# Block 0's transposed h by 32x32 transposes and transfers, and two steps of block 2 ahead of its first FFN chunk

## The chip, the cores and the metric

The kernel runs on one core of one Trainium2 chip. The core has TensorE (in the profile PE for matmuls, PEld for weight loads), VectorE (DVE), ScalarE (ACT), GpSimd (POOL) and SyncE (SP, which here only issues transfers). Each engine works through its own list of instructions in order, and the lists are coupled by semaphores alone. The metric is the device time in microseconds, the median of several runs.

## The reference

One transformer layer over 8192 tokens of 256 features: chunked linear attention with a decay mask and a gate, a residual and a layer norm, then a gated FFN with 768 hidden features and weights that are integers from -127 to 127, a residual and a second layer norm. Cut to its core:

```python
x = layernorm(x + attn(x)); x = layernorm(x + ffn(x))

# attn: T in chunks of C = 32
Q, K, V = x @ W_q.T, x @ W_k.T, x @ W_v.T
mask = where(i >= j, decay ** (i - j), 0)
S = einsum('bncd,bnkd->bnck', Qc, Kc) * mask
O = einsum('bnck,bnkd->bncd', S, Vc)
out = sigmoid(x @ W_g.T) * O @ W_o.T + x

# ffn
h = silu(x @ wg.T) * (x @ wu.T)
return h @ wd.T          # wg, wu, wd: integers / 127
```

## The kernel before

**Tiling.** The tokens are cut into 16 blocks of 512 (NB = 16, TB = 512). A block lies either with features on the partitions (two slices of 128 features, 512 tokens long; names with a T) or with tokens on the partitions (four groups of 128 tokens, 256 features long). The attention reads x in both layouts from memory; Q and K are folded into one product, y. Its steps for one block are v, y and the gate (each by Strassen's scheme of seven half-size products instead of eight, `seven`, L477), the scores (`attn_scores`, L611), the values times the gate (goT, L634) and the output projection with the residual. `seven` is called in two halves: the first issues four products and their sums, the returned function ("rest") issues the other three. Its inputs are sums of quarters of x or goT, which POOL makes (`token_sums`, L431).

**From attention to FFN.** After the residual, h is normalized and has to be turned, since the FFN wants features on the partitions. It is also split in two, hi in a rounded 32-bit format and lo, the remainder, in 16 bits; each FFN product is then done once with hi and once with lo. There are two ways of turning h. `transpose_h` (L710) lets TensorE transpose eight 128x128 tiles into two PSUM banks (tile pt), from where ACT writes hi and DVE writes lo. `move_h` (L729) lets DVE transpose within 32x32 squares (tile sq) and then has SP issue sixteen transfers of 32 KB that bring the squares to their places (tile hT); `split_h` (L752) then makes hi on ACT and lo on POOL. Before, block 0 and the last block go the first way, blocks 1 to 14 the second. Both sq and hT have one buffer.

**The normalization** also has two forms. `layer_norm` (L329) takes moments on DVE, a square root on ACT, a reciprocal on DVE, and scales on DVE, four times 128x256. `scale_and_shift` (L355) makes columns scale and shift on POOL, and `normalize` (L399) lets ACT apply them. `iterated_scale_and_shift` (L370) does the inverse root wholly on POOL, with a power and one refining step; block 1's h uses it (tiles v_h, y_h, t_h, minus_mean_h, term_h). A square root and a sigmoid need different ACT tables, so each change between them loads one.

**The FFN.** `ffn_up` (L768) takes one of six chunks of 128 hidden features: eight matmuls for gate (fg) and up (fu), hi and lo; even chunks begin with hi, odd ones with lo. ACT takes the sigmoid, DVE multiplies twice, and the product u is split like h, hi on ACT (L803), lo on POOL (L804). `ffn_down` (L816) multiplies back.

**Order.** The work is software-pipelined by hand: the FFN of block b stands beside the attention of block b+2 and the early products of block b+3. The prologue is L892 to L930, the loop L941 to L1026. A planner then orders each engine's list by its own idea of when things are ready, so the order in a list can differ from that in the code. `in_turn` (L293) pins an instruction behind the one that was traced before it on its engine; `in_steady_turn` does so only from the second turn of the loop on. A list, once made, is followed strictly: an instruction that waits holds up all behind it on its engine. In the prologue, block 0's output and norm come at L915, block 1's scores at L916, block 2's early products from L919, the turning of block 0 at L924, the load of the sigmoid table at L925, block 1's output from L927, and block 2's gate at L928. In the loop's first turn, chunk 0 is at L953, the gate's rest and block 3's token sums at L955, chunk 1 at L957, block 2's scores at L958 and the load of block 4's xT at L960.

Of the kernel before, what the change touches and what calls it, by code (L numbers as in the profile page):

```python
# [51 lines left out]
AF = mybir.ActivationFunctionType  # L52
ALU = mybir.AluOpType
# [13 lines left out]
HALF = 0.5  # L67
# [4 lines left out]
def kernel(  # L72
# [15 lines left out]
    nc = tc.nc  # L88
# [4 lines left out]
    NB = NT // TB  # L93
# [26 lines left out]
    def load_xT(b, start=None, pieces=1):  # L120
        xt = xin.tile([P, KD, TB], F32, tag="xT", name=f"xT_{b}")
        src = xT[:, span(b, start)].rearrange("(k p) t -> p k t", p=P)
        n = KD // pieces
        for k in range(0, KD, n):
            queue(start).dma_start(xt[:, k : k + n, :], src[:, k : k + n, :])
        return xt
# [15 lines left out]
    xTs, xns = {}, {}  # L142
# [44 lines left out]
    eps = const.tile([P, 1], F32, tag="eps", name="eps")  # L187
# [105 lines left out]
    def in_turn(ins):  # L293
        tc.keep_in_program_order(ins)
# [75 lines left out]
    def iterated_scale_and_shift(mv, kind, name):  # L370
        on_r, on_dst = kind

        def column(tag):
            return small.tile([P, NG], F32, tag=tag, bufs=2, name=f"{tag}_{name}")

        def times(out, a, b):
            nc.gpsimd.tensor_tensor(out, a, b, ALU.mult)

        def line(out, a, slope, at_0):
            nc.gpsimd.tensor_scalar(out, a, slope, at_0, ALU.mult, ALU.add)  # L380

        v, y, t, minus, shift = map(
            column, ("v", "y", "t", "minus_mean", "term")
        )
        in_turn(
            nc.vector.tensor_scalar(
                v, mv[:, :, 1], 1 / on_dst**2, EPS * (on_r / on_dst) ** 2, ALU.mult, ALU.add
            )
        )
        nc.gpsimd.tensor_tensor(y, v, half, ALU.pow)  # L390
        nc.gpsimd.tensor_scalar(minus, mv[:, :, 0], -1.0, None, ALU.mult)
        times(t, y, y)
        times(t, t, v)
        line(t, t, -0.5, 1.5)
        times(y, y, t)
        times(shift, y, minus)
        return y, shift
# [33 lines left out]
    def token_sums(t, name, order=free):  # L431

        out = sums.tile([P, 4, HB], F32, tag=f"{name[0]}_sums", name=f"{name}_sums")
        t1, t3, t2, t4 = (out[:, i, :] for i in range(4))
        b11, b12, b21, b22 = (t[:, k, n * HB : (n + 1) * HB] for k in range(2) for n in range(2))
        order(nc.gpsimd.tensor_tensor(t1, b12, b11, ALU.subtract))
        nc.gpsimd.tensor_tensor(t3, b22, b12, ALU.subtract)
        nc.gpsimd.tensor_tensor(t2, b22, t1, ALU.subtract)
        nc.gpsimd.tensor_tensor(t4, t2, b21, ALU.subtract)
        return b11, b21, b22, t4, t1, t2, t3  # L440
# [110 lines left out]
    def split_v(b, x_sums):  # L551
        v = work.tile([P, NG, D], F32, tag="v", name=f"v_{b}")
        return v, seven(f"v_{b}", token_major(w_sums["v"], x_sums), by_tokens(v))
# [57 lines left out]
    def attn_scores(b, yT):  # L611
        xt = xTs.pop(b)
        halves = [slice(i * PAIR, (i + 1) * PAIR) for i in range(P // PAIR)]
        ps = bank(f"ps_{b}")[:, : NG * PAIR].rearrange("p (g c) -> p g c", c=PAIR)
        for g in range(NG):
            for fc in range(KD):
                for rows in halves:
                    tokens = slice(g * P + rows.start, g * P + rows.stop)
                    nc.tensor.matmul(  # L619
                        ps[rows, g, :],  # L620
                        lhsT=xt[:, fc, tokens],
                        rhs=yT[:, fc, tokens],
                        start=(fc == 0),
                        stop=(fc == KD - 1),
                    )
        sTs.append(sTs.pop(0))
        sT = sTs[-1]
        for rows in halves:
            in_steady_turn(
                nc.vector.tensor_tensor(sT[rows, :, rows], ps[rows], mask[rows], ALU.mult)  # L630
            )
        return sT.rearrange("p g c -> p (g c)")
# [59 lines left out]
    def attn_out(b, goT):  # L692
        r = attn_residual(b, goT)
        layer_norm(r, f"a{b}", on_r=HALF, on_dst=H_UP)
        return r
# [216 lines left out]
    goT = attn_values(0, sT, v, sg)  # L912
    rest()
    fd = integers(ffn_dT, ffn_int[2], "fd")
    hs[0] = attn_out(0, goT)  # L915
    sT_1 = attn_scores(1, yT)  # L916
    xTs[3] = load_xT(3)
    x_sums = token_sums(xTs[2], "x_2")
    v, rest = split_v(2, x_sums)  # L919
    goT = attn_values(1, sT_1, v_1, sg_1)  # L920
    go_sums = token_sums(goT, "go_1")
    rest()
    yT, rest = split_y(2, x_sums)
    hTs[0] = transpose_h(0, hs[0])  # L924
    in_turn(nc.scalar.activation(table, eps, AF.Sigmoid))  # L925
    rest()
    hs[1], out_rest = split_out(1, go_sums)  # L927
    sg, g_rest = split_gate(2, x_sums)  # L928
    scales_h = iterated_scale_and_shift(out_rest(), of_h, "h_1")
    ahead = yT, v, sg  # L930

# [9 lines left out]
    for b in range(NB - 2):  # L941
        n = b + 2
        m = b + 3
        more = m < NB
        xns[n] = load_xn(n)
        hT = hTs.pop(b)
        uT = [], []
        yT, v, sg = ahead
        steady = b > 0
        if b:  # L950
            normalize(hs[b + 1], *scales_h)
            moving = move_h(b + 1, hs[b + 1])
        ffn_up(b, hT, uT, range(0, 1))  # L953
        if b == 0:
            g_rest()  # L955
            x_sums = token_sums(xTs[m], f"x_{m}")
        ffn_up(b, hT, uT, range(1, 2))  # L957
        sT = attn_scores(n, yT)  # L958
        if m + 1 < NB:
            xTs[m + 1] = load_xT(m + 1)  # L960
        ffn_up(b, hT, uT, range(2, 3))
        if b == 0:

            normalize(hs[b + 1], *scales_h)
            moving = move_h(b + 1, hs[b + 1])
        if not more:
            normalize(r_before, *scales_out)
            store(b - 2, r_before)
        if more:
            v_next, v_rest = split_v(m, x_sums)  # L970
        multiply = ffn_up(b, hT, uT, range(3, 4), held=True)
        if more:
            v_rest()
        multiply()
        goT = attn_values(n, sT, v, sg)
        if scales_out is not None and more:
            normalize(r_before, *scales_out)
            store(b - 2, r_before)
        if b == 0:
            look_up(range(4, n_pieces))  # L980
        if b == 1:
            count = count_wide()
        if more:
            go_sums = token_sums(goT, f"go_{n}")
            y_next, y_rest = split_y(m, x_sums)
        ffn_up(b, hT, uT, range(4, KH))
        r_before = r_out
        if more:
            y_rest()
            sg_next, g_rest = split_gate(m, x_sums)  # L990
            hs[n], out_rest = split_out(n, go_sums)
            g_rest()
            mv_h = out_rest()
            ahead = y_next, v_next, sg_next
            hTs[b + 1] = split_h(b + 1, moving)
            std_h = root_in_turn(mv_h, of_h, f"h_{b}")
            if b:
                mv_before, std_before = mv_out, root_in_turn(mv_out, of_out, f"out_{b}")
            back_to_sigmoids()
            if m + 1 < NB:  # L1000

                x_sums = token_sums(xTs[m + 1], f"x_{m + 1}", in_turn)

            def between():
                return scale_and_shift(mv_h, std_h, of_h, f"h_{b}")

            r_out, mv_out, scales_h = ffn_down(b, uT, hs.pop(b), between)
            if b:
                scales_out = scale_and_shift(mv_before, std_before, of_out, f"out_{b}")
        else:  # L1010

            hs[n] = attn_residual(n, goT)
            mv_h = moments(hs[n], f"a{n}", order=in_turn)
            std_out = root_in_turn(mv_out, of_out, f"out_{b}")
            hTs[b + 1] = split_h(b + 1, moving)
            std_h = root_in_turn(mv_h, of_h, f"h_{b}")
            back_to_sigmoids()
            scales_out = scale_and_shift(mv_out, std_out, of_out, f"out_{b}")
            normalize(r_before, *scales_out)
            store(b - 1, r_before)  # L1020

            inverse(std_h, slice(0, NG), HALF)
            for g in range(NG):
                by_vector(hs[n], g, mv_h, std_h)
            r_out, mv_out, _ = ffn_down(b, uT, hs.pop(b), chunkwise=True)
            scales_out = iterated_scale_and_shift(mv_out, of_out, f"out_{b + 1}")  # L1026


# [216 lines left out]
```

## Time and profile before

| | |
|---|---|
| median of 3 runs | 526.34 us (525.77 to 526.76) |
| the profiled execution | 526.4 us |
| its span, first to last instruction | 524.8 us |
| mean granted TensorE clock | 0.997 |
| TensorE matmuls busy | 517.6 us (99%) |
| DVE, POOL, ACT busy | 389.8, 343.0, 322.3 us |
| transfers, mean over the span | 70 GB/s |
| block 0's residuals added (DVE) | 32.20 to 34.61 us |
| block 0's transposes on TensorE | from 41.64 us |
| first FFN chunk on TensorE | from 48.58 us |

The profile is of one execution; its times count from the span's start. A line of the timeline has the start, the length, the engine with the line of the code, the operation, what it writes and reads with sizes, and, in brackets, how long the engine was idle before and what ended that. The chain of work that ended last is followed backwards from the last instruction. Ends of matmuls are modelled, so the chain, which cuts them to a sequence, is better for lengths on TensorE than the timeline, where neighbours overlap: it has the transposes at 41.81 and the first chunk at 48.83.

### The profile page before, as it was taken

The numbers are of one execution on the slowest core, as the hardware profiler recorded it, in microseconds if no ns is written. First come the engines' busy times: TensorE is split into PE (matmuls) and PEld (weight loads), VectorE is DVE, ScalarE is ACT, GpSimd is POOL, SyncE is SP. The second block draws the span as 40 slices with busy tenths as digits, with TensorE's granted clock in tenths as the row PEclk, the third lists the DMA queues.
The fourth block names the chain that finished last, engine by engine and source line by source line (L and its number), as shares of the span: only waits on it lengthen the run. The fifth ranks groups of instructions, "written<-read, shape, count | busy, mean of one in ns | idle before, by whom it ended". The sixth has DMA issues, their size and how long they took to land.

```text
span 524.8 us, 10553 instructions
## 1 busy us (share of the span) xinstructions
PE 517.6 (99%) x3646; PEld 422.3 (80%) x3646; DVE 389.8 (74%) x964; ACT 322.3 (61%) x644; POOL 343.0 (65%) x476
## 2 busy tenths in 40 slices
PE   8999999999999999999999999999999999999995
PEld 4798887887978789787888878879787888878684
DVE  3868797676776867868677776867868677787876
ACT  2754655475655766666665665656567566667745
POOL 6535785776857669486685856678486685835564
PEclk9999999999999999999999999999999999999998
DMA  8631111212313131121311413141131311102112
GB/s 259 197 107 41 49 42 46 67 41 56 108 30 91 49 112 42 38 91 51 105 42 43 120 25 97 44 116 43 33 91 51 110 42 39 44 21 61 44 38 84
DMA packets 43256, 36.90 MB, mean 70 GB/s; under 512 B 4800, under 2 KB 39104, under 8 KB 43200
## 3 DMA queue, kind: packets, MB, share of 16 engines
q1 hardware_dynamic: 42240, 35.41, 23.0%
q10 hardware_dynamic: 960, 0.79, 0.4%
q8 instruction: 30, 0.49, 0.4%
q14 instruction: 26, 0.21, 0.1%
HBM read 20.45 MB, written 8.39 MB: 55 GB/s over the span
## 4 chain that ended last, share of the span: by engine, by line
PE 96%; DVE 2%; ACT 1%; POOL 1%; issue 0%; DVEq 0%; ACTq 0%
PE fg L779 16%; PE fu L779 16%; PE fdn L666 14%; PE p_v L465 9%; PE p_y L447 9%; PE p_g L447 9%; PE p_o L465 8%; PE po L640 5%; PE ps L619 3%; PE fdn L845 2%; PE pa L666 1%; PE pg L561 1%; PE pi L183 1%; PE pv L599 1%; PE py L578 1%; DVE st_f L314 0%
## 5 line engine op out<-in xcount | busy, mean ns | idle before, releaser
L804 POOL TENSOR_TENSOR u_lo<-u,u_hi 128x512 f16<-128x512 f32 (+1 forms) x98 | 123.0, 1257 | 111.1 <-ACT u_hi L803 109.6
L803 ACT CAST u_hi<-u 128x512 fp32r<-128x512 f32 (+1 forms) x98 | 59.7, 609 | 65.3 <-DVE u L801 64.9
L789 DVE SCALAR_TENSOR_TENSOR s<-fg,s 128x512 f32<-128x512 f32 (+1 forms) x98 | 65.8, 673 | 34.3 <-ACT s L787 34.1
L787 ACT ACTIVATE s<-fg 128x512 f32<-128x512 f32 (+1 forms) x98 | 56.9, 583 | 41.5 <-PE fg L779 41.4
L801 DVE TENSOR_TENSOR u<-fu,s 128x512 f32<-128x512 f32 (+1 forms) x98 | 66.4, 678 | 10.4 <-POOL u_lo L804 1.1
L779 PE MATMUL fg<-hT_hi,fg_hi 128*128 128x512 f32 (+1 forms) x196 | 74.0, 458 | 0.0
L779 PE MATMUL fu<-hT_hi,fu_hi 128*128 128x512 f32 (+1 forms) x196 | 60.5, 390 | 0.0
L779 PE MATMUL fg<-hT_lo,fg_lo 128*128 128x512 f16 (+1 forms) x196 | 58.0, 377 | 0.0
L779 PE MATMUL fu<-hT_lo,fu_lo 128*128 128x512 f16 (+1 forms) x196 | 57.4, 375 | 0.0
L666 PE MATMUL fdn<-fd_hi,u_hi 128*128 128x256 f32 x312 | 46.9, 292 | 0.0
L779 PEld LDWEIGHTS fu<-hT_hi,fu_hi 128*128 128x128 f32 x196 | 36.5, 188 | 8.5
L402 ACT ACTIVATE h<-h,shift_h,scale_h 128x256 f32<-128x256 f32 x52 | 27.0, 590 | 24.1 <-POOL shift_h L365 24.1
L779 PEld LDWEIGHTS fg<-hT_hi,fg_hi 128*128 128x128 f32 x196 | 34.6, 189 | 8.8
L666 PEld LDWEIGHTS fdn<-fd_hi,u_hi 128*128 128x128 f32 x312 | 39.8, 189 | 0.3
L666 PE MATMUL fdn<-fd_lo,u_lo 128*128 128x256 f16 x312 | 38.6, 273 | 0.0
L779 PEld LDWEIGHTS <-fu_lo 128*128 128x128 f16 x196 | 19.2, 98 | 22.2
L827 DVE SCALAR_TENSOR_TENSOR r<-fdn,h 128x512 f32<-128x512 f32 x30 | 20.7, 689 | 21.6 <-PE fdn L666 19.1
L762 POOL TENSOR_TENSOR hT_lo<-hT,hT_hi 128x512 f16<-128x512 f32 x28 | 35.2, 1279 | 1.2 <-ACT hT_hi L761 1.2
L779 PEld LDWEIGHTS <-fg_lo 128*128 128x128 f16 x196 | 15.3, 98 | 20.6 <-issue 12.9
L666 PEld LDWEIGHTS <-u_lo 128*128 128x128 f16 x312 | 28.4, 98 | 4.2
L465 PE MATMUL p_v<-v_sums,x_sums 128*128 128x128 f32 x240 | 31.7, 275 | 0.0
L640 PE MATMUL po<-sT,v 128*128 128x128 f32 x256 | 31.2, 275 | 0.0
(207 smaller groups left out, 1183.4 us busy)
## 6 DMA issues: line engine op xcount, KB each, us to landing
x<-in_x_dram SPq DMA_DIRECT2D x16, 512.0 KB, 3.5
xT<-in_xT_dram SPq DMA_DIRECT2D x15, 512.0 KB, 4.2
hT<-sq SPq DMA_DIRECT2D x224, 32.0 KB, 1.9
out_dram<-r SPq DMA_DIRECT2D x14, 512.0 KB, 4.5
fg_int<-in_ffn_gT_dram SPq DMA_DIRECT2D x3, 256.0 KB, 8.4
fu_int<-in_ffn_uT_dram SPq DMA_DIRECT2D x3, 256.0 KB, 7.1
fd_int<-in_ffn_dT_dram SPq DMA_DIRECT2D x3, 256.0 KB, 5.8
xT<-in_xT_dram SPq DMA_DIRECT2D x2, 256.0 KB, 4.2
```

The lines of the kernel that those rows point to most:

```text
L402: nc.scalar.activation(r[:, g, :], r[:, g, :], AF.Identity, bias=shift[:, g : g + 1], scale=scale[:, g : g + 1],)
L447: nc.tensor.matmul(pb, lhsT=a[i - 1], rhs=b[i - 1], start=first, stop=True, skip_group_check=True,)
L465: nc.tensor.matmul(pb[:, g * P : (g + 1) * P], lhsT=b[i - 1][:, g * P : (g + 1) * P], rhs=a[i - 1], start=first and g == 0, stop=True, ski ...
L640: nc.tensor.matmul(po[:, cols], lhsT=v[:, g, dc * P : (dc + 1) * P], rhs=sT[:, cols], start=True, stop=True,)
L666: nc.tensor.matmul(pb[:, j * D : (j + 1) * D], lhsT=part[:, g * P : (g + 1) * P], rhs=w, start=(i == 0), stop=(i == len(terms) - 1),)
L762: nc.gpsimd.tensor_tensor(in_order[1], whole, in_order[0].bitcast(F32), ALU.subtract)
L779: nc.tensor.matmul(pb, lhsT=w[kind][:, dc, hc * P : (hc + 1) * P], rhs=hT[kind][:, dc, cols], start=(kind == kinds[0] and dc == 0), stop=( ...
L787: order(nc.scalar.activation(s, pg, AF.Sigmoid, scale=SCALE / H_UP))
L789: gated = nc.vector.scalar_tensor_tensor(s, pg, U_UP / H_UP**2, s, ALU.mult, ALU.mult)
L801: in_steady_turn(nc.vector.tensor_tensor(u, pu, s, ALU.mult))
L803: nc.scalar.copy(hi, u)
L804: nc.gpsimd.tensor_tensor(lo, u, hi.bitcast(F32), ALU.subtract)
```

## The change

Block 0 goes the way of the other blocks. A table load for the square root comes first; `attn_residual`, the moments, `root` and `scale_and_shift` take the place of `attn_out`; after block 2's first v products ACT normalizes, loads the sigmoid table, and `move_h` issues transposes and transfers. `split_h` comes after block 2's first gate products, where hTs[0] is now made.

In the loop's first turn the gate's rest, block 3's token sums, block 2's scores and the load of block 4's xT come before chunk 0 instead of after chunks 0 and 1. In later turns their order is as it was.

Three more instructions on POOL are pinned: in `iterated_scale_and_shift` the power (behind whatever was traced before it) and the negated mean (behind the power), for every use of it; and in `token_sums` the second sum, t3, wherever the caller gives an order. That is so at the end of each turn, and now in the first turn too.

```diff
-        nc.gpsimd.tensor_tensor(y, v, half, ALU.pow)
-        nc.gpsimd.tensor_scalar(minus, mv[:, :, 0], -1.0, None, ALU.mult)
+        in_turn(nc.gpsimd.tensor_tensor(y, v, half, ALU.pow))
+        in_turn(nc.gpsimd.tensor_scalar(minus, mv[:, :, 0], -1.0, None, ALU.mult))
...
         order(nc.gpsimd.tensor_tensor(t1, b12, b11, ALU.subtract))
-        nc.gpsimd.tensor_tensor(t3, b22, b12, ALU.subtract)
+        order(nc.gpsimd.tensor_tensor(t3, b22, b12, ALU.subtract))
...
-    hs[0] = attn_out(0, goT)
+    in_turn(nc.scalar.activation(table, eps, AF.Sqrt))
+    hs[0] = attn_residual(0, goT)
+    mv_h = moments(hs[0], "a0")
+    std_h = root(mv_h, "a0", HALF)
     sT_1 = attn_scores(1, yT)
+    scales_h = scale_and_shift(mv_h, std_h, of_h, "h_0")
     xTs[3] = load_xT(3)
     x_sums = token_sums(xTs[2], "x_2")
     v, rest = split_v(2, x_sums)
+    normalize(hs[0], *scales_h)
+    in_turn(nc.scalar.activation(table, eps, AF.Sigmoid))
+    moving = move_h(0, hs[0])
     goT = attn_values(1, sT_1, v_1, sg_1)
     go_sums = token_sums(goT, "go_1")
     rest()
     yT, rest = split_y(2, x_sums)
-    hTs[0] = transpose_h(0, hs[0])
-    in_turn(nc.scalar.activation(table, eps, AF.Sigmoid))
     rest()
     hs[1], out_rest = split_out(1, go_sums)
     sg, g_rest = split_gate(2, x_sums)
+    hTs[0] = split_h(0, moving)
     scales_h = iterated_scale_and_shift(out_rest(), of_h, "h_1")
...
-        hT = hTs.pop(b)
...
+        else:
+            g_rest()
+            x_sums = token_sums(xTs[m], f"x_{m}", in_turn)
+            sT = attn_scores(n, yT)
+            xTs[m + 1] = load_xT(m + 1)
+        hT = hTs.pop(b)
         ffn_up(b, hT, uT, range(0, 1))
-        if b == 0:
-            g_rest()
-            x_sums = token_sums(xTs[m], f"x_{m}")
         ffn_up(b, hT, uT, range(1, 2))
-        sT = attn_scores(n, yT)
-        if m + 1 < NB:
-            xTs[m + 1] = load_xT(m + 1)
+        if b:
+            sT = attn_scores(n, yT)
+            if m + 1 < NB:
+                xTs[m + 1] = load_xT(m + 1)
```

## Prediction

> **What bounds the kernel now.** I read the page's busy shares first, then the chain of work that ended last around the edit, then busy time by stage.
>
> ```profile
> PE 517.6 (99%) x3646; PEld 422.3 (80%) x3646; DVE 389.8 (74%) x964; ACT 322.3 (61%) x644; POOL 343.0 (65%) x476
> ...
> 34.00:42.00 8.00, 8.00 (x88) 7.67 (x87) 6.99 (x19) 3.34 (x7) 1.88 (x3) 1.00 0.39 133
> 48.00:54.00 6.00, 6.00 (x41) 4.18 (x41) 4.83 (x17) 2.71 (x6) 3.74 (x7) 1.00 0.27 87
> ```
>
> The columns of the last two lines are the stage, its length, then busy time of PE, PEld, DVE, ACT and POOL, granted clock, DMA share and GB/s. TensorE has no gap in either stage: each microsecond of matmul taken away there is a microsecond of the kernel, and each microsecond for which TensorE waits is added. The other four engines have room. The chain in order of time says the same, and gives the pieces the edit touches (start, length, what):
>
> ```profile
> 41.81 0.87 PE pt L718 x8
> ...
> 48.83 0.47 PE fg L779 x2
> ...
> 50.21 0.43 PE fu L779 x2
> 50.64 1.29 PE p_g L447 x6
> ...
> 53.73 1.08 PE ps L619 x32
> ```
>
> So the eight transposes of block 0 cost TensorE 0.87 us. The first chunk of block 0's FFN runs 48.83 to 50.64 (1.81 us), the gate's rest takes 1.29, block 2's scores 1.08.
>
> The new way of moving h is already used for blocks 1 to 14. Block 2's move, in the timeline:
>
> ```profile
> 83.53 0.20 POOL L365 TENSOR_TENSOR shift_h<-mv_a,minus_h 128x4 f32<-128x4 f32 x1
> 83.76 2.08 ACT L402 ACTIVATE h<-h,shift_h,scale_h 128x256 f32<-128x256 f32 x4 [3.14 <-POOL shift_h L365]
> ...
> 84.39 1.92 DVE L737 STREAM_TRANSPOSE sq<-h 128x256 f32<-128x256 f32 x4 [0.85 <-ACT h L402]
> ...
> 86.39 11.32 SPq L744 DMA_DIRECT2D hT<-sq  x16
> ```
>
> And the split that follows it, of block 1, with the landing time of all such transfers from the view of tile sq:
>
> ```profile
> 76.04 1.12 ACT L761 CAST hT_hi<-hT 128x512 fp32r<-128x512 f32 x2
> ...
> 78.34 2.52 POOL L762 TENSOR_TENSOR hT_lo<-hT,hT_hi 128x512 f16<-128x512 f32 x2
> ...
> DMA to landing us min/median/max: 1.8/1.9/3.7
> ```
>
> To be seen: first DMA issue 2.63 us after the normalization starts; sixteen issues one behind another on SP, 11.3 us here (10.34, 11.06, 10.73, 10.19 for the other four of the first five, median 10.7); 1.9 us from an issue to its landing; then 0.6 us for the first hi half and 2.5 us for both lo halves. In blocks 1 to 14 some 24 us lie between normalization and first use. Block 0 hasn't got them.
>
> **What the Trainium skill says.** "VectorE: DVE Perf Modes", The three transpose paths: VectorE transposes only inside 32x32 blocks. So the rest of the move is the DMAs' work, sixteen per block here. "DMA: Bandwidth & Descriptors", Bandwidth: transfers under 64 KB are governed by their descriptors, not their bytes. The trace agrees: 32 KB each, 0.6 us of SP each. "ScalarE: Activation LUTs", What ACT_TABLE_LOAD costs: about 1283 ns; the trace has 1.28 us at 36.04. "TensorE: Matmul & The Clock Gate", Part 1: after an idle window of about 3.4 us the clock is halved. The trace shows only the warm-up: the four L183 matmuls of 128x512 start 0.86 us apart where such steps later take 0.43.
>
> **The change part by part.**
>
> Transposes gone from TensorE: -0.87 us. With them go two ACT reads of pt (1.08 us) and two DVE lo halves (1.29), off the path.
>
> Normalization moved from VectorE to ScalarE: four L338 (2.02 us) and one L336 off DVE; four ACTIVATEs (2.08) onto ACT, three small POOL operations. Table loads stay two, one moved forward to about 33 us, when ACT has been through the fd casts and idles until 35.65; one table activation (0.20) is new. Hidden by ACT's idle time; without it, about 2.3 us of delay, not on TensorE's queue.
>
> When does h leave? The last aggregate ends at 35.88, the root takes 0.30 with its table already there, ready by about 36.3. The reciprocal is held behind block 1's second masking (35.91 to 36.34), so 36.37 to 36.55. Three POOL operations take 0.58 (83.15 to 83.73 in the trace of before), so the normalization starts at 37.2. First issue 2.63 later: 39.8. Attention's goT multiply (0.69) becomes ready in the midst of the transposes and can get between them: from 0 to 1.0, I take 0.4. First issue 40.2.
>
> Sixteen DMAs on SP, otherwise empty from 35.6 to 48.5: the last is issued 10.1 us after the first (10.7 less its own 0.6), 50.3, and lands 1.9 later, 52.2. The first hi half 0.61: 52.85. Two lo halves on POOL 2.52: 55.4. What of chunk 0 then remains, three steps of 0.22: chunk 0 ends at 56.05.
>
> What is queued behind these waits: behind each transpose on DVE goT, v and y of the early products; behind the hi casts on ACT the gate's sigmoids; behind the lo halves on POOL, now by an explicit pin, block 1's power and all its scale chain, and behind that block 3's token sums. Delay before chunk 0 costs nothing as long as TensorE still arrives before h, so the lost 0.87 us of cover between y's two halves (copies and p57 may come late by up to 0.5) is free.
>
> The order of TensorE: it would arrive at chunk 0 at 48.83 - 0.87 + 1.29 + 1.08 = 50.33. Before, the same set (chunk 0, gate's rest, scores) was done at 48.83 + 1.81 + 1.29 + 1.08 = 53.01. Now 56.05. Net so far **+3.0 us**: a stall of 3.9 less 0.87.
>
> The pins on POOL: pow starts at 55.4, 1.05; minus 0.2; five small ones at 0.28 apiece, done 58.05; then t1, t3, t2 at 0.74, t2 at 60.3. TensorE, after chunks 1 and 2 (1.79 each), needs t2 after v's first product (0.45): 60.1. So +0.2 to +0.3 there. At worst a u_lo (1.28) gets in ahead: +1.5. In blocks 1 on, pinning t3 puts it behind the lo halves instead of ahead (it ran at 77.66, before 78.34): same POOL total, and TensorE never waited. In the tail minus goes behind pow in the chain at 507: same work, 0 to 0.1.
>
> The steps moved ahead. The gate's rest issues three ACT operations (0.38, 0.42, 0.63), two DVE sums and the token sums. The ACT ones may queue behind the hi casts until 53.5 and end at 55; their first user, block 2's attention multiply, ran at about 64. The scores issue two DVE maskings (0.43 each), used as late. The load of block 4's xT is released by the scores and goes onto SP behind the sixteen issues, which end at about 51; before it was issued at 54.85, and its user comes 25 us later. Block 3's x load, at 48.46 before, may wait on SP until 51 too; its user comes at about 75. Tiles sq and hT have one buffer each: block 1's transposes (60.0) and transfers (62.4) need block 0's landed (52.2) and split (55.4). All at nothing, with 2 us or more to spare.
>
> Sum: -0.87 + 3.9 + 0.3 = **+3.3**. The profiled execution took 526.4 (span 524.8), the median is 526.34: predicted **529.6**.
>
> **The rivals.**
>
> A, likeliest, as above: +3.3; with the first issue from 39.8 to 40.8, the issue train from 10.2 to 11.3 and the sums' stall from 0 to 0.4, +2.1 to +4.6. Chance 0.47.
>
> B, the planner lets other matmuls into the gap. The first products of v, y and g of block 3 read the raw xT (0.45, 0.43, 0.43 us), chunk 2's hi products 0.93. They aren't pinned. For it: in the old schedule t3 ran ahead of the lo halves, so the planner thinks these late. Against it: nowhere in the old trace does TensorE run ahead of its program order. Gives +1.0 to +2.4; 528.2. Chance 0.25.
>
> C, A and something on top: the u_lo ahead of the sums, or the clock halved. The longest unbroken idle is 2.5 us, below the skill's window, but TensorE is busy for only 0.9 in 5. An estimate from the page: half speed for 3.4 us, +1.7. Gives 531.2 to 532. Chance 0.17.
>
> D, not slower: the move is hidden. Place: SP's sixteen issues. It decides if the last lands by about 48.5, so that both lo halves are there when chunk 0 wants them (51.5); that needs the train to take under 7 us, where the trace never shows less than 10.2. Price: -0.87, 525.5. Chance 0.08. The last 0.03 is for disturbances I don't see.
>
> That the pins fail to hold the order (scores behind chunk 0 again) would only lengthen the stall; it is in C.
>
> **How the numbers follow.** Within 0.2% (1.05 us) is about what a measurement of this kernel can't tell from no change. A, C and nearly all of B are above it: slower 0.88. D is 0.16% below before, so it counts as the same: 0.09 with B's lower edge. Faster needs more than the 0.87 that is there to be had: 0.03. For 8 in 10 I leave out D (0.08), B's lowest third (0.08) and C's upper end (0.04): 527.8 to 531.8. A's own range is 528.4 to 530.9.
>
> **What would show it.** No pt on TensorE. ACT normalizing h of block 0 at about 37, before the sigmoid table. SP issuing hT from about 40.2 to 51. ACT's hT_hi at about 52.2, waiting for the DMA. TensorE idle before the first fg of block 0 at about 50.3 to 52.9, and a second time, for hT_lo on POOL, until 55.4. Block 3's x_sums finished about 61 instead of 56.15. The prediction is wrong if the hT issues end before 47, if TensorE runs block 3's products in that gap, or if the difference to before grows again after 62, in stages I called covered.

## The result, and the profile after

The changed kernel takes 532.59 us (median of 5 runs, 531.88 to 533.75) against 526.54 beside it: ratio 1.0122, interval 1.0111 to 1.0134. The forecast was 529.6 with a range of 527.8 to 531.8; the sign was right, and 3 us were missing. The profiled execution took 532.59 (span 530.95; before 526.4 and 524.81), so 6.1 us are to be found in the span. They lie in two places, 470 us apart.

**The first place is block 0's first chunk.** From the page of the changed kernel, the busy shares; then the same two stages as in the prediction and three short ones (stage, length, busy time of PE, PEld, DVE, ACT, POOL, granted clock, DMA share, GB/s), and last two of the short ones in the kernel before:

```profile
PE 518.2 (98%) x3638; PEld 421.5 (79%) x3638; DVE 391.6 (74%) x961; ACT 322.7 (61%) x649; POOL 345.7 (65%) x481
```

```profile
34.00:42.00 8.00, 8.00 (x81) 7.67 (x78) 7.18 (x20) 5.76 (x14) 3.47 (x8) 1.00 0.44 140
48.00:54.00 6.00, 3.78 (x42) 2.42 (x41) 3.40 (x14) 2.36 (x5) 1.69 (x2) 0.97 0.50 148
...
53.00:55.00 2.00, 1.38 (x5) 0.56 (x5) 0.00 (x0) 0.60 (x2) 2.00 (x3) 0.65 0.94 340
55.00:57.00 2.00, 2.00 (x6) 0.62 (x5) 0.77 (x2) 0.60 (x1) 1.75 (x6) 0.50 0.03 8
57.00:58.00 1.00, 1.00 (x6) 0.77 (x5) 0.61 (x1) 0.00 (x0) 0.92 (x4) 1.00 0.00 0
```

```profile
53.00:55.00 2.00, 2.00 (x37) 1.52 (x36) 0.65 (x2) 1.32 (x3) 2.00 (x4) 1.00 0.03 8
55.00:57.00 2.00, 2.00 (x12) 1.27 (x12) 1.39 (x4) 1.00 (x2) 1.84 (x7) 1.00 0.49 94
```

From 48 to 54 TensorE is busy for 3.78 of 6 us, where before it had no gap; and from within 53:55 until 57 it runs at half its clock, which it had not done before. The timeline shows block 0's h on its way:

```profile
37.00 2.08 ACT L402 ACTIVATE h<-h,shift_h,scale_h 128x256 f32<-128x256 f32 x4 [0.27 <-POOL shift_h L365]
...
39.85 10.34 SPq L744 DMA_DIRECT2D hT<-sq  x16
...
51.62 1.14 ACT L761 CAST hT_hi<-hT 128x512 fp32r<-128x512 f32 x2 [3.05 <-DMA hT<-sq]
...
52.29 1.02 PE L779 MATMUL fg<-hT_hi,fg_hi 128*128 128x512 f32 x2 [2.19 <-ACT hT_hi L761]
...
52.31 2.51 POOL L762 TENSOR_TENSOR hT_lo<-hT,hT_hi 128x512 f16<-128x512 f32 x2 [4.33 <-ACT hT_hi L761]
...
54.87 0.59 PE L779 MATMUL fg<-hT_lo,fg_lo 128*128 128x512 f16 x1 [0.62 <-POOL hT_lo L762]
```

And the chain of work that ended last (start, length, what) runs through SP's queue, the last transfer, both halves of the split, and into products of which a pair takes 0.85, twice the usual 0.43:

```profile
49.59 1.85 DMA hT<-sq
...
52.31 2.52 POOL hT_lo L762 x2
54.83 0.04 issue
54.87 0.59 PE fg L779
55.46 0.85 PE fu L779 x2
56.31 0.84 PE fg L779 x2
57.15 0.43 PE fu L779 x2
```

By block 0's products back (fdn) the loss is 3.53 us, before and then after in the chain:

```profile
76.28 5.52 PE fdn L666 x48
```

```profile
79.81 5.52 PE fdn L666 x48
```

Block 0's output projection (tile pa) starts at 30.43 before and 30.20 after in the chain, so from pa to fdn it is 45.85 us before and 49.61 after. It stays there: the last compute of all, the copy of n_wide, comes 3.58 later.

```profile
521.62 0.13 DVE L1179 CAST n_wide<-count 1x1 int32<-1x1 f32 x1
```

```profile
525.20 0.13 DVE L1189 CAST n_wide<-count 1x1 int32<-1x1 f32 x1
```

**The second place is behind the last compute**, where the span goes on for 3.06 us before and 5.61 after, 2.6 us more. Behind n_wide every engine loads that number and branches over the code for wide integers (`tc.If`, L1183 before, L1193 after). The view of that line, before and then after (count, shortest, median and longest in ns, start):

```profile
L1183 ACTq COMPARE_BRANCH  x1: 45/45/45, 522.5 to 522.5; - x1
...
L1183 PEldq COMPARE_BRANCH  x1: 445/445/445, 522.6 to 522.6; - x1
```

```profile
L1193 ACTq COMPARE_BRANCH  x1: 45/45/45, 526.1 to 526.1; - x1
...
L1193 PEldq COMPARE_BRANCH  x1: 3658/3658/3658, 526.2 to 526.2; - x1
```

TensorE's branch takes 3.66 us instead of 0.45, and the other engines wait for it at the end. "Runtime: NRT & Kernel Launch", Instruction fetch mechanics, in the Trainium skill, says that instructions are fetched 16 KB at a time, in sequence, and that a taken branch to a place not among the loaded ones has to wait for a fetch. It gives no time. The trace agrees as far as it shows fetches: the DMA view of the 8 us ahead of TensorE's branch has one on TensorE's instruction queue before,

```profile
q8 instruction: 1, 0.02, 1.0%
```

and none after the change; there two follow the start of the branch, where before it was one (view from 526.2 to 531):

```profile
q8 instruction: 2, 0.03, 2.9%
```

(Columns: fetches, MB, share. The view doesn't name the engine of q8. Over the whole trace it has 30 fetches, 0.49 MB, one for some 245 of TensorE's records, and it is taken for TensorE's queue from that.) The change takes transposes from TensorE: its stream has 16 records fewer, 3638 matmuls and as many weight loads instead of 3646. So the theory to test: **the stream's length moves the branch against the fetches, and the 2.6 us have nothing to do with h.** The rival: something moved by the change (pins, loads) makes the end late. For the first place the theory is the late h, and on top of it the half clock.

### The profile page after: what moved, and what is told of

Its sections match the earlier page's. It is cut to its first block, busy times and chain, and to the rows that moved or that the text cites. A ratio compares the mean times of both kernels' runs of the same rounds, so it can differ in the third digit from the quotient of the medians.

```text
span 531.0 us, 10574 instructions
## 1 busy us (share of the span) xinstructions
PE 518.2 (98%) x3638; PEld 421.5 (79%) x3638; DVE 391.6 (74%) x961; ACT 322.7 (61%) x649; POOL 345.7 (65%) x481
## 4 chain that ended last, share of the span: by engine, by line
PE 90%; DVE 3%; SPq 2%; POOL 1%; DMA 1%; ACT 1%; issue 0%; DVEq 0%; ACTq 0%
PE fg L779 16%; PE fu L779 15%; PE fdn L666 14%; PE p_v L465 8%; PE p_y L447 8%; PE p_g L447 8%; PE p_o L465 8%; PE po L640 5%; PE ps L619 3%; PE fdn L845 2%; SPq L744 2%; PE pa L666 1%; DMA wg<-in_w_gT_dram 1%; PE pg L561 1%; PE pv L599 1%; PE py L578 1%
## 5 line engine op out<-in xcount | busy, mean ns | idle before, releaser
L787 ACT ACTIVATE s<-fg 128x512 f32<-128x512 f32 (+1 forms) x98 | 55.7, 581 | 41.4 <-PE fg L779 40.2
L402 ACT ACTIVATE h<-h,shift_h,scale_h 128x256 f32<-128x256 f32 x56 | 29.1, 590 | 26.2 <-POOL shift_h L365 26.2
L762 POOL TENSOR_TENSOR hT_lo<-hT,hT_hi 128x512 f16<-128x512 f32 x30 | 37.7, 1279 | 9.3 <-ACT hT_hi L761 9.3
```

The costliest lines, as they stand in the source:

```text
L402: nc.scalar.activation(r[:, g, :], r[:, g, :], AF.Identity, bias=shift[:, g : g + 1], scale=scale[:, g : g + 1],)
L762: nc.gpsimd.tensor_tensor(in_order[1], whole, in_order[0].bitcast(F32), ALU.subtract)
L787: order(nc.scalar.activation(s, pg, AF.Sigmoid, scale=SCALE / H_UP))
```

## Experiments on the end

**Length restored in the warm-up.** `idle` is a tile of zeros, `pi` the warm-up's bank.

```diff
+    for _ in range(4):
+        nc.tensor.matmul(pi[:, :32], lhsT=idle[:, :P], rhs=idle[:, :32], start=True, stop=True)
```

> The changed kernel with four float32 matmuls of 128x32 added to the warm-up, so that TensorE's stream has again the 3646 matmul and 3646 weight-load records of the kernel before. They run in the first microseconds, where TensorE has nothing else to do. Theory (the branch): the end of the changed kernel is 2.65 us longer only because TensorE's closing branch took 3.66 us instead of 0.45, and that depends on the length of the stream alone; here the branch is back near 0.45 us, the stretch from the last compute (n_wide) to the end near 3.05 us, and the time at about +3.5 us over the kernel before (530.0, ratio 1.0067). Rival (the tail comes from the pins on GpSimd, or from the moved loads): the stretch stays at 5.7 us and the time at +6 us (ratio 1.0115).

Measured: 533.45 us, ratio 1.0143 (1.0126 to 1.0161), branch 3.54 us. A miss: as many matmuls as before, and a long branch still.

**Length cut in the kernel before.** It leaves out the second half of the features in the scores of block 15's first 256 tokens.

```diff
+                if b == NB - 1 and g < 2 and fc:
+                    continue
...
-                        stop=(fc == KD - 1),
+                        stop=(fc == KD - 1 or (b == NB - 1 and g < 2)),
```

> The kernel before, with a part of the computation left out: the second half of the features in the scores of block 15's first 256 tokens (four float32 products), so that TensorE's stream is 8 matmul and 8 weight-load records shorter, as the changed kernel's is. Nothing of the change is in it. Theory (the branch): the closing branch takes about 3.66 us and the stretch behind the last compute about 5.7 us, which with about 0.2 us of work left out gives +2.4 us (529.0, ratio 1.0046). Rival (the change itself causes the tail): the stretch stays at 3.05 us and the time at -0.2 us (ratio 0.9996).

Measured: 528.68 us, ratio 1.0042 (1.0027 to 1.0057), branch 3.78 us. As the theory says, and against the rival: 16 records of matmuls and weight loads fewer in the kernel before, nothing else of the change, cost 2.6 us net between the medians (528.68 and 526.1).

**Five instead of four in the warm-up.**

> The changed kernel with five instead of four float32 matmuls of 128x32 in the warm-up. The padded kernel with four kept the long branch (3.54 us) and has 7378 records on TensorE's two queues; the kernel before and the filled one have 7379 and a short branch (0.45 and 0.46 us). Theory (the length of TensorE's stream decides, and the step lies between 7378 and 7379): here there are 7382, the branch takes about 0.45 us, the stretch behind n_wide about 3.05 us, and the time is +3.4 us over the kernel before (529.5, ratio 1.0064; 1.005 to 1.0075). Rival (the branch depends on what the changed part does, and the filled kernel shortened it by its faster part): the branch stays near 3.6 us and the ratio at 1.0115 to 1.014.

Measured: branch 0.455 us, with a fetch ahead of it. But 531.64 us, ratio 1.0088 (1.0073 to 1.0103): only part of the gain. The timeline says why: the small matmuls aren't free, and in this execution the eight products behind them took 5.60 us instead of 3.82 in the changed kernel; pa came 3.5 us later than there (33.69 in the chain). TensorE was at the half pace of the warm-up until about 11 us: the weight loads of these products start 0.85 us apart up to 10.80 and 0.43 apart from 11.40, and the clock's record has it full from 11.1, where the changed kernel has it from 5.8. It doesn't always go so: with six small matmuls, in the kernel below that moves h alone, the products took 3.68.

```profile
5.25 2.18 PE L185 MATMUL pi<-idle 128*128 128x32 f32 x10
7.25 5.60 PE L563 MATMUL pg<-xT,wg 128*128 128x512 f32 x8
```

That was a fault of the experiment: padding needs a place where TensorE is really free. Behind its last product it is, for some 3 us.

```diff
+    last = bank("last")
+    for _ in range(5):
+        in_turn(nc.tensor.matmul(last[:, :32], lhsT=idle[:, :P], rhs=idle[:, :32], ...))
     n_wide = const.tile([1, 1], I32, tag="n_wide", name="n_wide")
```

> The changed kernel with five float32 matmuls of 128x32 behind TensorE's last product, where it only waits for n_wide (7382 records, as in the kernel with five in the warm-up). In the warm-up they were not free: block 0's first product behind them (pa) began 0.1 to 3.5 us later than in the changed kernel, and the times fell into two groups 2 us apart. Theory (the branch costs 2.65 us of the change's 6.2, the pads in the warm-up cost the rest): branch 0.45 us, one group of times, +3.5 us over the kernel before (529.9, ratio 1.0067; 1.0055 to 1.0075). Rival (the spread belongs to the changed kernel): two groups again, a median ratio of 1.009.

Measured: 532.33 us, ratio 1.0125 (1.0109 to 1.014), branch 3.40 us. A miss again, though the stream has the records of the kernel with five in the warm-up. Ten, and then seven, in the same place:

> The changed kernel with ten instead of five small matmuls behind the last product (7396 records before the branch against 7376). Theory (the fetch of the next 16 KB of instructions comes ahead of the branch once the stream is long enough): a fetch on TensorE's instruction queue some 8 us before the branch, branch 0.45 us, +3.5 us over the kernel before (529.6, ratio 1.0067; 1.0055 to 1.008). Rival (only records ahead of the fetch's place count, and those behind the last product don't): as with five, branch 3.4 us and ratio 1.0125.

> The changed kernel with seven small matmuls behind the last product (7384 records before the branch), to place the step between five (7376, long) and ten. Theory (a step at a fixed number of records): short (0.45 us) if the step lies below 7384, as the kernels with 7380 and 7381 records and a short branch say. Rival (records behind the last product don't count): long (3.4 us).

Ten: 530.2 us, ratio 1.0073 (1.006 to 1.0085), branch 0.445. Seven: branch 3.52 (one run, 533.49 us).

```profile
L1198 PEldq COMPARE_BRANCH  x1: 445/445/445, 528.1 to 528.1; - x1
```

All kernels together, in the order of the records (matmuls, weight loads and the few others) that TensorE has in the trace ahead of its branch; the first expectations, with 7378 and 7379, count six behind it as well:

| kernel | records | fetch in the 8 us ahead | branch, us |
|---|---|---|---|
| changed; before, cut | 7356; 7357 | no | 3.66; 3.78 |
| four in the warm-up; two queues | 7372 | no | 3.54; 3.78 |
| before; filled | 7373 | yes | 0.45; 0.46 |
| five in the warm-up | 7376 | yes | 0.46 |
| five at the end; sums first | 7376 | no | 3.40; 3.49 |
| order alone; pins alone | 7377 | yes | 0.45; 0.45 |
| x later; early and vector; h alone | 7380; 7380; 7381 | yes | 0.46; 0.45; 0.45 |
| seven at the end | 7384 | no | 3.52 |
| ten at the end, both kernels | 7396 | yes | 0.45; 0.46 |

In all 17 kernels a fetch ahead of the branch and a short branch go together. Among the kernels with nothing added at the end, the longer streams (from 7373 on) have it and the shorter ones (up to 7372) not, so the kernel before stood within a few records of the step. What is shown is that records which compute nothing decide 2.1 to 2.4 us (the changed kernel without and with ten: medians 532.59 and 530.2; each set against the kernel before beside it, +6.05 and +3.9). What stays open is the rule of the step: 7384 records were not enough with seven matmuls at the end, where 7373 were in the kernel before. Something that this count misses takes part.

## Experiments on the wait for h

**The wait filled.** Four float32 matmuls between the scores and chunk 0.

```diff
+            fill = bank("fill")
+            for _ in range(4):
+                in_turn(nc.tensor.matmul(fill, lhsT=idle[:, :P], rhs=idle, start=True, stop=True))
         hT = hTs.pop(b)
```

> The changed kernel with four float32 matmuls of 128x512 (of the warm-up's constants, into a bank that nobody reads) between block 2's scores and block 0's first chunk, where TensorE waited 2.19 us. The stream has the length of the kernel before, as in the padded kernel. Theory (the clock): the half clock from about 53 to 58 us, about 1.2 us of the stall, came of TensorE's idle stretch; with the stretch filled the products of chunk 0 run at 0.21 us from the start, and the time is about 1.2 us below the padded kernel's: +2.3 us over the kernel before (ratio 1.0044). Rival (the clock falls there whatever TensorE does, or the filling takes as long as it saves): the same as the padded kernel, +3.5 us (ratio 1.0067).

Measured: 529.15 us, ratio 1.0057 (1.0044 to 1.007). The branch is short here, so the kernel to set beside it is the one with ten at the end: 1.05 us between the medians, though the intervals of the two ratios overlap. The filled kernel's stages:

```profile
53.00:55.00 2.00, 2.00 (x8) 0.98 (x7) 0.00 (x0) 0.83 (x2) 2.00 (x2) 1.00 1.02 360
55.00:57.00 2.00, 1.99 (x10) 1.10 (x9) 0.74 (x2) 0.60 (x1) 1.83 (x6) 1.00 0.09 31
```

Full clock throughout, with useless work: TensorE's idling cost about 1 us beyond the idling itself. The traces agree: from pa to fdn it is 48.63 us here, against 49.61 in the changed kernel, in whose chain the three pieces at half clock are 0.37, 0.42 and 0.41 longer, 1.2 us. The price isn't the same in each execution: in the five kernels that only have small matmuls added, from pa to fdn it is 48.8 to 51.3 us.

The ratio is above the expected 1.0044, mostly because the kernel with a short branch is itself at +3.8 us and not at +3.5. The filling's length costs little: it runs on until 53.94, while h's first half was ready at 52.5, but TensorE comes to the second low half at 55.10, and POOL has it ready at 55.06 (chain, then timeline):

```profile
55.10 0.01 issue
55.12 0.38 PE fg L779
```

```profile
52.54 2.52 POOL L762 TENSOR_TENSOR hT_lo<-hT,hT_hi 128x512 f16<-128x512 f32 x2 [4.34 <-ACT hT_hi L761]
```

**h's new way alone**, with the gate's rest and the scores back at their places behind chunks 0 and 1:

> The changed kernel with six small matmuls in the warm-up (short branch) and with the gate's rest and block 2's scores back at their places of the kernel before, behind chunks 0 and 1. Theory (the moved work is what covers the transfers): 1.5 us of the gate's rest and 1.15 us of scores no longer lie in the wait, so the wait at the first chunk grows from 2.2 to about 4.8 us and the time is +6.0 us over the kernel before (ratio 1.0114; 1.009 to 1.0135). Rival (the planner finds other work for the wait, or the order is worth nothing): as the kernel with five small matmuls, +3.4 us (ratio 1.0064).

Measured: 535.24 us, ratio 1.0172 (1.0146 to 1.0197). The wait is the 4.8 that was expected, nearly; the time is 3 us more than expected. Its four runs lie at 533.56, 533.88, 536.6 and 537.06, and the profile is that of the second.

```profile
52.78 0.79 PE L781 MATMUL fg<-hT_hi,fg_hi 128*128 128x512 f32 x1 [4.55 <-ACT hT_hi L763]
```

```profile
55.00:57.00 2.00, 1.96 (x5) 0.92 (x4) 0.40 (x1) 0.60 (x1) 1.86 (x5) 0.50 0.00 0
57.00:59.00 2.00, 2.00 (x6) 1.48 (x5) 0.76 (x3) 0.40 (x2) 0.59 (x3) 0.50 0.00 0
```

The half clock is longer here too: it lasts from 52.4 (mean 0.94 in 48:53) to 59.2 (0.95 in 59:61), 6.8 us; in the changed kernel from 53.6 to 57.0, 3.4 us. In the profiled execution of the kernel with ten at the end it was 6.8 us as well (54.2, from 0.79 in 53:55, to 61.0, from 0.75 in 60:62), and that run took 532.03 us where the five others took 529.83 to 531.57, three of them under 529.9. So a longer wait isn't needed for it. The six small matmuls in the warm-up of h alone may have added to its upper two runs.

In all eight traces that have a half clock at this place it lasts 3.4 or 6.8 us. The changed kernel's own five runs fit this: those with a mean granted clock of 0.994 took 531.88 to 532.59, those with 0.991 took 533.44 and 533.75. (In the kernel with ten at the end one run of 531.57 has 0.997 and doesn't fit.) In the clock's record of all 17 traces the stretches at full clock, too, are multiples of 3.41 us long: in seven of the eight the clock falls 47.8 us, 14 times 3.41, after it first rose. So the clock seems to change only at every 3.41 us counted from its first rise, and the place of the wait between two such points may decide how long the half clock is. No run here moves the one against the other alone, so that is not shown.

So the moved work covers 2.4 us of the wait (2.19 against 4.55), and the change without it would be worse.

**The two other parts alone,** each in the kernel before with one small matmul at the end.

> The kernel before with the three instructions on GpSimd pinned, as the change pins them, and nothing else of it (one small matmul behind the last product keeps TensorE's stream at no less than 7379 records). Theory (the pins decide nothing by themselves; the changed kernel's end waits 0.2 us for u_lo at the last products because of them): 0 to +0.2 us, branch 0.45 us (ratio 1.0 to 1.0005). Rival (the pins order GpSimd worse in every block): +1 us or more (ratio 1.002).

> The kernel before with the gate's rest, block 3's token sums, block 2's scores and the load of xT put ahead of block 0's first chunk, h still moved by TensorE (one small matmul behind the last product). Theory (the new order itself costs nothing; the loss is in how h is moved): -0.3 to 0 us, as three switches between the scores and chunk products fall away (ratio 0.9994 to 1.0). Rival (the later start of the chunks leaves VectorE and GpSimd idle, and u or the sums come late): +0.4 us or more (ratio 1.0008).

Measured: pins 526.5 us, ratio 1.0006 (0.9997 to 1.0014); order 526.6, ratio 1.0006 (0.9998 to 1.0015). Neither differs measurably from no change; the pins' rival (1.002) is excluded, that of the order (1.0008) isn't. The pins' trace has one wait more than that of before, 0.2 us at the very last products, as all kernels with the pins have it:

```profile
PE fdn L1092 <- POOL u_lo L804: 0.2, 1, 0.2
```

From pa to fdn it is 45.86 us in both traces, as before (45.85). With that, the loss in block 0 belongs to the late h, since only the kernels that move h have the wait for it.

## Experiments on what makes h late, and a faster version

**Two queues.** ACT's queue issues five of the sixteen transfers (`issue_later` takes them from a list).

```diff
-    moving = move_h(0, hs[0])
+    moving = move_h(0, hs[0], [(2, 3)] + [(3, j) for j in range(4)])
...
     rest()
+    issue_later(2)
     hs[1], out_rest = split_out(1, go_sums)
     sg, g_rest = split_gate(2, x_sums)
+    issue_later(3)
```

> The padded kernel, with five of block 0's sixteen transfers issued from ScalarE's queue (two behind y's rest, three behind the gate's copies) and eleven from SP's. Theory (the stall is the length of the queue: sixteen issues in 10.34 us, 0.65 us apart): the last transfer lands about 3.2 us earlier, the casts begin at about 48.5 to 49.5 us, TensorE waits under 1 us, the clock is not halved, and the time is about +0.4 us over the kernel before (ratio 1.0008; 0.9995 to 1.002). Rival (the transfers themselves or VectorE's squares are what is late, or the two queues slow each other): the stall stays, +2.5 to +3.5 us (ratio 1.005 to 1.0067).

Measured: 532.62 us, ratio 1.0138 (1.0108 to 1.0168). A miss. SP's part was over early, yet h came no earlier. The timeline of this kernel, and the landing times of block 0's tile hT (us, shortest, median, longest):

```profile
40.50 7.13 SPq L753 DMA_DIRECT2D hT<-sq  x11
...
46.64 1.94 ACTq L760 DMA_DIRECT2D hT<-sq  x3
...
48.00 0.37 SPq L131 DMA_DIRECT2D x<-in_x_dram  x1
...
52.31 1.14 ACT L771 CAST hT_hi<-hT 128x512 fp32r<-128x512 f32 x2 [3.08 <-DMA hT<-sq]
```

```profile
DMA to landing us min/median/max: 1.9/1.9/4.2
```

SP, free at 47.6, sent off the next thing in its list: block 3's x, 512 KB. The last small transfers, issued until 48.6, then took up to 4.2 us instead of 1.9 (longest for block 0 in the changed kernel: 2.4). A faster queue had started what it collided with, if this reading is right. Block 3's x held back until block 1's transfers are issued, the load of block 4's xT pinned where it is traced, and six small matmuls in the warm-up in place of four:

```diff
-        xns[n] = load_xn(n)
+        xns[n] = load_xn(n, order=in_turn if b == 1 else free)
...
-            xTs[m + 1] = load_xT(m + 1)
+            xTs[m + 1] = load_xT(m + 1, order=in_turn)
```

> The kernel with two queues, with six small matmuls in the warm-up in place of four (short branch), and with block 3's x, whose load SP issued at 48.0 us between the transfers on ScalarE's queue, held behind block 1's transfers. In the kernel with two queues the last issue was over at 48.6 us but the first cast came at 52.3. Theory (the x load of 512 KB took the DMA engines while the last three transfers were on their way: 4.2 us to landing instead of 1.9): the casts begin at 50.3 to 50.7 us, TensorE waits about 0.5 to 1 us, the clock stays full, and the time is +0.9 us over the kernel before (ratio 1.0017; 1.0005 to 1.003). Rival (two queues slow each other, whatever else moves): casts near 52.3 us, +3.3 us (ratio 1.0063).

Measured: 529.29 us, ratio 1.0047 (1.0029 to 1.0065). In its trace, which is 3.1 us behind that of the two queues from the warm-up on (again the small matmuls), the last issue was over at 51.65, ACT's last three landed in 1.9 us at most, and the cast followed in 1.4 us instead of 3.7:

```profile
49.71 1.94 ACTq L760 DMA_DIRECT2D hT<-sq  x3
...
53.09 1.14 ACT L771 CAST hT_hi<-hT 128x512 fp32r<-128x512 f32 x2 [0.80 <-DMA hT<-sq]
```

So the collision was the cause. The time missed its mark, by the warm-up and by a wait of 0.84 us for POOL's second low half, behind which the clock stayed full. Next, ACT's issues earlier and that half on DVE:

> As the kernel before this one in the list, with the five transfers on ScalarE's queue earlier (three behind y's rest, one behind the p_o copies, one behind the p_g copies) and block 0's second low half computed on VectorE instead of GpSimd (about 0.65 us there against 1.28). Theory (all the loss of the changed kernel but the branch is the late hT): the casts begin at about 49.5 us, TensorE waits under 0.3 us, and what is left is the gain of the change, 0.87 us of transposes: -0.6 us against the kernel before (ratio 0.9989; 0.998 to 1.0). Rival (the added issues delay ScalarE's copies of the sums and so TensorE, or the order costs elsewhere): +0.5 us or more (ratio 1.001).

Measured: 527.41 us, ratio 1.0039 (1.0027 to 1.0052); its lower runs are at 526.7 to 527.5, the others, ten of 22, at 529.6 to 531. In its profile, one of the lower runs, TensorE no longer waits for h, but for what POOL puts off for it:

```profile
PE p_v L467 <- POOL x_sums L440: 0.4, 1, 0.4
```

**The fastest version:** block 3's token sums ahead of the inverse root on POOL, the small matmuls at the end.

```diff
     hTs[0] = split_h(0, moving)
+    x_sums = token_sums(xTs[3], "x_3", in_turn)
     scales_h = iterated_scale_and_shift(out_rest(), of_h, "h_1")
...
-            x_sums = token_sums(xTs[m], f"x_{m}", in_turn)
```

> The kernel with the early transfers and VectorE's low half, with the small matmuls moved from the warm-up to behind the last product, and block 3's token sums put ahead of the inverse root's steps on GpSimd, where p_v waited 0.37 us for them. Theory (what was left of its +0.6 us was 0.5 us of small matmuls at the start, 0.37 us of this wait and 0.2 us of u_lo at the end, against a gain of 0.9 us): about -0.3 to -0.7 us against the kernel before (525.8, ratio 0.999; 0.998 to 1.0003), one group of times. Rival (another wait comes up in place of the sums, u_lo of block 0's first chunk or the normalization of block 1): +0.3 us or more (ratio 1.0006).

Measured: 528.09 us, ratio 1.004 (1.0026 to 1.0053): a miss, but n_wide came 1.27 us earlier than in the kernel before (0.49 of it lay ahead of pa already, at 29.94), and the branch was long, 3.49 us. With ten at the end:

> The kernel with the token sums first, with ten instead of five small matmuls behind the last product. In its run the last compute (n_wide) came at 520.35 us, 1.27 us earlier than in the kernel before, but the branch took 3.49 us and no fetch of 16 KB on TensorE's instruction queue lay between 508 and 522 us. Theory (with enough records the fetch comes ahead of the branch): branch 0.45 us, -1.0 us against the kernel before (525.0, ratio 0.998; 0.9965 to 0.999). Rival (records behind the last product don't count for the fetch): branch 3.4 to 3.8 us, +2 us as with five (ratio 1.004).

Measured: **525.61 us, ratio 0.9986 (0.9979 to 0.9992)**, branch 0.46: 0.7 us faster than the kernel before (526.3 beside it), and 7 us than the changed one. In its chain the first chunk follows the scores with no wait, at full clock:

```profile
49.22 1.08 PE ps L619 x32
50.30 0.67 PE fg L788 x2
50.97 0.46 PE fu L788 x2
51.44 0.45 PE fg L788 x2
```

Block 0's fdn starts at 75.41 instead of 76.28, 0.87 us earlier, with pa at 30.41: the 0.87 us of the transposes, which this change can give if h arrives in time.

## Why the prediction was wrong, and where it was right

- **The step that failed is the tail, put at "0 to 0.1" and left out of the sum.** It looked at the work of the tail and had no term for the code behind it. That TensorE's stream gets 16 records shorter could be read from the diff; that the kernel ends in a branch over skipped code could be read from the profile of before, where TensorE's branch took 445 ns and the others' 45 to 72. The term measures 2.6 us in the trace (5.61 against 3.06 behind n_wide) and 2.1 to 2.4 between medians. It alone took the time out of the range: without it the time would be about 530.
- **The half clock was mis-sized as an alternative.** The prediction saw that TensorE would be busy for little in that stretch, but kept the slowdown for C (0.17) at +1.7, because no single idle stretch reached the skill's 3.4 us ("TensorE: Matmul & The Clock Gate", Part 1). The longest was 2.19 us, and the clock still fell, at 53.6, some 3.5 us after the idling began, with TensorE at work from 52.3 on. Price 1.0 to 1.2 us in the profiled execution. It belonged in the sum.
- **The stall itself was right.** Normalization at 37.0 (predicted 37.2), first issue 39.85 (40.2), lo halves done at 54.8 (55.4); a goT multiply did get between the transposes. The changed kernel ran 0.23 us ahead at 30 us already (pa), so h came 0.3 us ahead of the forecast on the old kernel's clock. The forecast's +3.0 at this place less 0.3, plus 1.1 for the clock, is 3.8; measured 3.53 + 0.23 = 3.8.
- **The sums' +0.3 was nothing here**, since TensorE came later than POOL; where TensorE didn't wait for h, it appeared at 0.37, in the place that was named. That +3.3 for this place came within 0.5 us is in part luck: h's 0.3 and these 0.3 went against the 1.1 of the clock.
- The reading that 0.6 us of SP per transfer is a matter of descriptors is not shown by any run. It isn't one of bytes: in the changed kernel the load of x, 512 KB, took SP 0.52 us at 50.30.
- B is refuted: TensorE ran nothing of block 3 in the gap. D failed at the place it named, SP's sixteen issues. The transposes' worth, 0.87, was exact.
- With a short branch the change is at +3.8 us (530.2), within A's own range of 528.4 to 530.9.

## What to carry to other kernels

Before costing an edit, look behind the last compute: a branch over unused code can cost microseconds that depend on how many instructions stand ahead of it. Equal counts didn't settle it here, so compare the length of the branch itself in both traces. A stall on TensorE can cost more than itself: a slower clock followed the wait of 2.19 us here, though not one of 0.84. And when a queue is shortened, look at what it issues next, because that goes out earlier too.

## What the runs showed of the hardware

- TensorE's closing branch takes 0.45 or 3.4 to 3.8 us, by whether a fetch of instructions came ahead of it; on the other engines the same branch takes 45 to 72 ns.
- The half clock came 3.5 us after the start of a wait of 2.19 us, with some 1.3 us of work behind the wait, and lasted 3.4 us, or 6.8 in other traces.
- With ten records of 128x32 matmuls at the end of the warm-up TensorE came to full clock at 11.1 us in place of 5.8 in one trace, and the eight products behind them took 5.60 us in place of 3.82; with twelve it was 4.6 us and 3.68 in another.
- In all 17 traces TensorE's granted clock changed only at multiples of 3.41 us from its first rise.
- A load of 512 KB issued in the midst of 32 KB transfers on another queue raised the longest landing among block 0's from 2.4 to 4.2 us; with the load held back, the last ones landed in 1.9.
